# Attention block with Fourier layer: the values' bias added on ScalarE instead of GpSimd

## The chip, the cores and the metric

The kernel runs on one core of a Trainium2 chip, as one launch. The metric is the device time of that launch in microseconds (us); several runs are taken and their median is compared. One execution is also recorded by the hardware profiler. The engines of a core are named as in the profile: PE (TensorE, its weight loads PEld), DVE (VectorE), ACT (ScalarE), POOL (GpSimd) and SP (SyncE, which here only issues transfers). Each engine works through its own queue in order and waits at semaphores for the others.

## The reference

The input is an image of 48 x 48 tokens with 768 channels. The first layer is a transformer block with 12 heads of 64 channels and relative positions, the second a Fourier layer on blocks of 96 channels. Cut to what matters here:

```python
xn  = layernorm(x)
qkv = xn @ qkv_w + qkv_b                    # q, k, v: 12 heads, 2304 tokens, 64 channels
attn = (q * scale) @ k.T + rel_h[..., None] + rel_w[..., None, :]
out = softmax(attn) @ v                     # 12 x 2304 x 64
x   = x + out @ proj_w + proj_b
x   = x + gelu(layernorm(x) @ mlp_w1 + mlp_b1) @ mlp_w2 + mlp_b2
# second layer: rfft2, two small block matrices with relu and softshrink, irfft2, plus x
```

The bias of the values is not added to the values. As the weights of a softmax sum to one, it is added to the finished output of attention: `softmax(attn) @ (v + b) = softmax(attn) @ v + b`. This addition is what the change moves.

## The kernel before, in words

All arithmetic is in float32. The kernel has these stages: normalisation with queries, keys and values (up to about 402 us in the profile), attention (402 to 1471 us), projection (to about 1609 us), the two layers of the MLP (to about 2628 us) and the Fourier layer (to the end). A general form of attention stands in a branch for inputs whose sums overflow; it isn't executed here.

**Attention.** Heads are taken in six pairs (`pr`), queries in six chunks of 384 (`c`), so there are 36 chunks, counted 0 to 35 in this document (chunk 6 is `pr` 1, `c` 0). A chunk works as follows.

- For each of 18 tiles of 128 keys, PE makes the scores of both heads into a bank `sp` of PSUM, of which there are three (L678 for the content, L687 for the position), and ACT writes their exponentials into `main` (L697, the activation function Exp). DVE adds the exponentials up in `pairs` two tiles at a time (L871), and at the end in `acc` (L875).
- Then PE multiplies the exponentials with the values into `op` (L710), in six steps of three key tiles. Between the steps the function `between` puts other work, in an order written out by hand (`work[0]` to `work[5]`).
- Part of this work is for later chunks. `relative` makes the row terms of the position for a chunk three ahead; `columns` makes the column terms of the next pair. Both go through `two_parts`: two copies on ACT (L248, L249) and a subtraction on DVE (L250). `in_columns` copies queries on ACT (L702). Each `relative` then issues 24 transfers on SP's queue (L317, L321) that fill the tile `terms`. There is one such set in chunks with `c` from 0 to 2 and `c` = 4, and two sets where `c` = 5; the last pair needs fewer.
- The rest is for the denominators. In step 1 DVE turns and sums `acc` into `part` (L728, L730). In step 4 PE adds up over the partitions (L739), DVE takes the reciprocal `rden` (L741, two buffers) and adds to `sums` (L742), and POOL adds `rden` to `inverse` (L743), by which overflow is recognised later. In step 5 SP writes `rden` to `den_d` in DRAM (L757), stores a finished chunk, whose product was made in the chunk before, (`stored`, L791), and spreads the denominators of the chunk before over the partitions by two transfers, `spread` (L770). DVE then multiplies the output of two chunks before by its `spread` into `o` (L782, two buffers), and the bias is added to `o` (L785).
- After the last step ACT copies `op` to `ot` (L751), and the exponentials of the next chunk follow in its queue.

The orders of ACT, DVE and POOL in attention and those of PE and SP are the program's own (`manual_schedule`); nothing is reordered by a scheduler.

**POOL's other work.** During attention POOL also prepares the weights of the MLP: 48 pieces, two a chunk. A piece is a load into the single buffer `seven` (`asked`, L802, issued on POOL's own queue), four additions or subtractions of 128 x 192 (`left` or `right`, L164 to L167 or L175 to L178) and a store to `w1_d` or `w2_d` (L815). POOL's order within a chunk is: load (`kt == 2`), sums and store (`kt == 12`), load (step 1), `inverse`, bias, sums and store (end of the chunk). The function that is changed, and the one that orders its place:

```python
4: [partial(inverses, pr, c)],
5: [partial(left_apart, pr, c), stored],
...
work[5] += [partial(spread_out, 1), partial(scaled, 1)]
```

Of the kernel before, what the change touches and what calls it, by code (L numbers as in the profile page):

```python
# [13 lines left out]
AF = mybir.ActivationFunctionType  # L14
ALU = mybir.AluOpType
# [27 lines left out]
V_LN1G, V_LN1B, V_LN2G, V_LN2B, V_QB, V_KB, V_VB, V_B1 = 0, 6, 12, 18, 24, 30, 36, 42  # L43
# [4 lines left out]
def block_then_afno(  # L48
# [27 lines left out]
    nc = tc.nc  # L76
# [15 lines left out]
    def col(i):  # L92
        return vec[:, i : i + 1]
# [102 lines left out]
    def by_rows(a):  # L196

        return a.rearrange("p (h b w) -> p b h w", h=8, b=3, w=16)

    def by_blocks(a):  # L200
        return a.rearrange("p (b h w) -> p b h w", h=8, b=3, w=16)

    with ExitStack() as flag_scope:
# [12 lines left out]
        with ExitStack() as att:  # L216
# [121 lines left out]
            def queries_keys_values(qkv):  # L338
# [263 lines left out]
                for p in range(T // TB):  # L602
# [13 lines left out]
                    for n, (kind, i) in enumerate(orders[p]):  # L616
                        if p < 2:
                            q = p + 1
                            if n in (5, 6):
                                hooks += [partial(centred, q, 3 * (n - 5) + c) for c in range(3)]  # L620
                            if n in (6, 7):
                                hooks[:0] = [partial(scaled, q, 3 * (n - 6) + c) for c in range(3)]
                            if n == 8:
                                hooks += [partial(token_sum, q, j) for j in range(4)]
# [36 lines left out]
            with tc.manual_schedule(engines={mybir.EngineType.PE, mybir.EngineType.SP}):  # L661
# [114 lines left out]
                def scaled(keep):  # L776

                    while len(to_scale) > keep:
                        pr, c, spread = to_scale.pop(0)
                        (ot,) = made.pop((pr, c))  # L780
                        o = o_pool.tile([P, G], F32, name="o")
                        nc.vector.tensor_tensor(  # L782
                            by_rows(o), by_blocks(ot), by_blocks(spread), ALU.mult
                        )
                        nc.gpsimd.tensor_scalar(o, o, col(V_VB + pr), None, ALU.add)  # L785
                        results.append((pr, c, o))

                def stored(queue=nc.sync):
# [28 lines left out]
                def between(pr, c, acc):  # L817

                    last = pr == NC - 1
                    work = {  # L820
                        1: [asked, partial(denominators, pr, c, acc)],
                        4: [partial(inverses, pr, c)],
                        5: [partial(left_apart, pr, c), stored],
                    }
                    if last and c > 2:
                        work[5] += [partial(spread_out, 0), partial(scaled, 1), stored]
                    else:
                        work[5] += [partial(spread_out, 1), partial(scaled, 1)]
                    if c < 3:
                        work[0] = [partial(relative, pr, c + 3)]  # L830
                    elif not last and c < 5:
                        for n in range(3):
                            work.setdefault(n, []).append(partial(columns, pr + 1, 3 * (c - 3) + n))
                        if c == 4:
                            work[3] = [partial(relative, pr + 1, 0)]
                    elif not last:
                        work[0] = [partial(relative, pr + 1, 1)]
                        work[2] = [partial(relative, pr + 1, 2)]
                    if not last and c in (2, 3):
                        for n in range(3):  # L840
                            i = 3 * (c - 2) + n
                            work.setdefault(n + (1, 3)[c - 2], []).append(
                                partial(in_columns, pr + 1, i)
                            )
                    return work
# [199 lines left out]
        with tc.If(safe < 1):  # L1045
            with ExitStack() as att:
# [27 lines left out]
                for pr in range(NC):  # L1074
# [12 lines left out]
                    for g in range(T // G):  # L1087
                        kp = psum.tile([P, G], F32, name="g_kp", tag="m")
                        for c in range(NC):
# [5 lines left out]
                            bias=kb[0:64, pr : pr + 1], scale=HD**-0.5,  # L1095
# [18 lines left out]
                    for sg in range(T // SG):  # L1114
# [4 lines left out]
                        for i in range(2):  # L1119
                            qp = psum.tile([P, G], F32, name="qp", tag="m")  # L1120
                            for c in range(NC):
# [6 lines left out]
                                bias=vec[0:64, V_QB + pr : V_QB + pr + 1],  # L1128
# [154 lines left out]
    with ExitStack() as mlp:  # L1283
        bias = mlp.enter_context(tc.tile_pool(name="mlp_const", bufs=1))
# [576 lines left out]
```

## Time and profile before

| | |
|---|---|
| median of 3 runs | 2881.7 us (2877.34 to 2889.69) |
| the profiled execution's own time | 2885.64 us |
| its span | 2883.8 us |
| granted clock of TensorE, mean | 0.991 |
| PE busy in the span | 2797.0 us (97%) |
| DVE busy | 1723.1 us (60%) |
| ACT busy | 920.0 us (32%) |
| POOL busy | 694.3 us (24%) |
| attention, first exponential to last copy `ot` | 403.7 to 1471.4 us |
| weight sums on POOL, first load to last store issued | 402.9 to 1187.6 us |

The span is the time from the first to the last recorded instruction. A busy share is an average over all stages; it does not say where an engine is waited for. The lists of waits say this: each line names an engine and a line that stood idle, then what released it, then the total in us, how often, and the longest. In the timelines a line gives the start, the duration, engine, source line and operation, and in brackets the idle time before it with its releaser. What is inferred there is the last event before the start; for a wait on several things it can name the wrong one. SPq lines are transfers issued by SP: their times are those of the issue, not of the transfer.

### The profile page before, as it was taken

The numbers are of one execution on the slowest core, as the hardware profiler recorded it, in microseconds if no ns is written. First come the engines' busy times: TensorE is split into PE (matmuls) and PEld (weight loads), VectorE is DVE, ScalarE is ACT, GpSimd is POOL, SyncE is SP. The second block draws the span as 40 slices with busy tenths as digits, with TensorE's granted clock in tenths as the row PEclk, the third lists the DMA queues.
The fourth block names the chain that finished last, engine by engine and source line by source line (L and its number), as shares of the span: only waits on it lengthen the run. The fifth ranks groups of instructions, "written<-read, shape, count | busy, mean of one in ns | idle before, by whom it ended". The sixth has DMA issues, their size and how long they took to land. (4 is left out here: it accounts for less than half of the span.)

```text
span 2883.8 us, 40970 instructions
## 1 busy us (share of the span) xinstructions
PE 2797.0 (97%) x15759; PEld 1717.5 (60%) x15759; DVE 1723.1 (60%) x2520; ACT 920.0 (32%) x1466; POOL 694.3 (24%) x662
## 2 busy tenths in 40 slices
PE   8999999999999899799999999999999999999998
PEld 4555655555656455465555555555555555556887
DVE  5434247667766566576766656675665556566665
ACT  1101136656656465475521210121110211112332
POOL 3405024445434344300045010011000100002433
PEclk9999999999999999899999999999999999999999
DMA  5535387585875867737352223223322322323254
GB/s 164 167 113 175 83 176 174 126 183 131 159 178 134 186 137 144 166 64 110 84 189 78 81 103 115 105 98 109 115 81 111 140 96 78 114 97 118 61 160 140
DMA packets 230716, 363.46 MB, mean 126 GB/s; under 512 B 26180, under 2 KB 203964, under 8 KB 224368
## 3 DMA queue, kind: packets, MB, share of 16 engines
q1 hardware_dynamic: 215720, 306.80, 40.2%
q0 software_dynamic: 12352, 52.11, 5.7%
q8 instruction: 127, 2.08, 0.3%
q10 hardware_dynamic: 2440, 1.84, 0.2%
q14 instruction: 77, 0.63, 0.1%
HBM read 211.59 MB, written 85.35 MB: 103 GB/s over the span
## 5 line engine op out<-in xcount | busy, mean ns | idle before, releaser
L697 ACT ACTIVATE main<-sp 128x768 f32<-128x768 f32 x648 | 516.3, 812 | 34.5 <-PE sp L687 19.3
L1320 PE MATMUL h<-shared,w 128*128 128x384 f32 x1512 | 504.1, 486 | 0.7 <-issue 0.7
L871 DVE TENSOR_TENSOR pairs<-pairs,main 128x1536 f32<-128x1536 f32 x252 | 461.7, 1832 | 27.1 <-DVE pairs L871 0.9
L687 PE MATMUL sp<-terms,select 64*128 64x384 f32 x1296 | 411.8, 629 | 0.0
L1320 PEld LDWEIGHTS h<-shared,w 128*128 128x128 f32 x1512 | 287.0, 190 | 202.0 <-issue 2.5
L1380 DVE TENSOR_TENSOR main<-o,main 128x384 f32<-128x384 f32 x540 | 299.1, 557 | 38.3 <-PE o L1378 0.2
L678 PE MATMUL sp<-shared 64*128 64x384 f32 x1296 | 264.6, 485 | 1.6 <-ACT row_hi L249 1.0
L678 PE MATMUL sp<-qT,kT 64*128 64x384 f32 x1296 | 264.2, 484 | 0.0
L1378 PE MATMUL o<-w,hs 128*128 128x384 f32 x648 | 262.6, 487 | 1.4 <-DVE hs L165 1.0
L1378 PE MATMUL o<-w,hT 128*128 128x384 f32 x648 | 245.2, 487 | 3.0 <-DVE main L1380 3.0
L1395 POOL TENSOR_TENSOR main<-main,acc 128x384 f32<-128x384 f32 x9 | 11.4, 1266 | 924.6 <-DVE main L1380 665.2
L710 PE MATMUL op<-main,shared 128*64 128x384 f32 x1296 | 222.7, 495 | 0.0
L710 PE MATMUL op<-main,v 128*64 128x384 f32 x1296 | 222.3, 496 | 0.0
L1326 ACT ACTIVATE hT<-c,vec 128x384 f32<-128x384 f32 x108 | 66.4, 615 | 465.2 <-DVE c L1332 465.1
L1332 DVE TENSOR_TENSOR c<-h,u 128x384 f32<-128x384 f32 x108 | 60.2, 558 | 212.8 <-PE h L1320 212.8
L871 DVE TENSOR_TENSOR pairs<-main 128x1536 f32<-128x1536 f32 x36 | 63.7, 1769 | 192.0 <-ACT main L697 192.0
L1378 PEld LDWEIGHTS o<-w,hT 128*128 128x128 f32 x648 | 122.7, 190 | 90.1 <-DVE main L1380 6.2
L1378 PEld LDWEIGHTS o<-w,hs 128*128 128x128 f32 x648 | 122.5, 190 | 89.4 <-DVE main L1380 4.8
L687 PEld LDWEIGHTS sp<-terms,select 64*128 64x128 f32 x1296 | 124.9, 186 | 84.1
L537 PE MATMUL m<-main 128*128 128x384 f32 x504 | 164.6, 488 | 2.2 <-DVE main L187 1.2
L710 PEld LDWEIGHTS op<-main,v 128*64 128x64 f32 x1296 | 99.1, 139 | 95.1 <-issue 71.5
L710 PEld LDWEIGHTS op<-main,shared 128*64 128x64 f32 x1296 | 98.1, 139 | 91.1 <-issue 67.1
(205 smaller groups left out, 3679.4 us busy)
## 6 DMA issues: line engine op xcount, KB each, us to landing
w<-w_d SPq DMA_DIRECT2D x72, 1344.0 KB
w_d<-seven POOLq DMA_DIRECT2D x48, 672.0 KB, 5.6
terms<-col_parts SPq DMA_DIRECT2D x432, 72.0 KB
seven<-in_w_blocks_dram POOLq DMA_DIRECT2D x48, 384.0 KB, 4.7
terms<-row_hi SPq DMA_DIRECT2D x216, 72.0 KB
terms<-row_lo SPq DMA_DIRECT2D x216, 72.0 KB
main<-in_qkv_w_dram SPq DMA_DIRECT2D x36, 384.0 KB
z<-zt SPq DMA_DIRECT2D x48, 192.0 KB
```

Source lines behind the costliest of these rows:

```text
L537: nc.tensor.matmul(bank, a[:, c, :], b[:, c, :], start=(first and c == 0), stop=(c == 2), skip_group_check=not first,)
L678: nc.tensor.matmul(sp[:, j, :G], kT[at, ts(kt, P)], qT[at, ts(c, G)], start=first, stop=not first,)
L687: nc.tensor.matmul(sp[:, j, :G], select[at, a % 2], ready[pr, c][at, a // 2, b], start=first, stop=not first,)
L697: nc.scalar.activation(p, sp[:, :, :G], AF.Exp, scale=HD**-0.5)
L710: nc.tensor.matmul(op[ts(j, 64)], v[:, kt, ts(j, 64)], exps[:, kt, j, :], start=(kt == 0), stop=(kt == NT - 1),)
L871: nc.vector.tensor_tensor(pairs, so_far, exps[:, ds(kt - 1, 2)], ALU.add)
L1320: nc.tensor.matmul(bank[i], a[:, c, :], b[:, c, :], start=(start and c == 0), stop=(c == 2), skip_group_check=not start,)
L1326: nc.scalar.activation(h[:, i, ts(k, G)], src, AF.Gelu, bias=col(V_B1 + tiles_of_chunk(n)[i]))
L1332: nc.vector.tensor_tensor(t, src, other, ALU.add)
L1378: nc.tensor.matmul(bank[k], a, b, start=start, stop=True, skip_group_check=not start)
L1380: nc.vector.tensor_tensor(dst, bank[k], dst, ALU.add)
L1395: nc.gpsimd.tensor_tensor(x12, x12, acc[i], ALU.add)
```

## The change

One line of the function `scaled`. The addition of the bias to the tile `o` (128 x 384, in place, one value of bias per partition) is now an activation with the function Identity on ACT; before it was a `tensor_scalar` on POOL. It stays at the same place of the program, so it stands in ACT's queue behind the copies of `two_parts` in that chunk and ahead of the copy `ot` (L751). In chunks with `c` 2 or 3 one of the copies of `in_columns` comes behind it as well. The orders of PE, DVE and SP are the same as before; the store of `o` waits for ACT and no longer for POOL.

```diff
                         nc.vector.tensor_tensor(
                             by_rows(o), by_blocks(ot), by_blocks(spread), ALU.mult
                         )
-                        nc.gpsimd.tensor_scalar(o, o, col(V_VB + pr), None, ALU.add)
+                        nc.scalar.activation(o, o, AF.Identity, bias=col(V_VB + pr))
                         results.append((pr, c, o))
```

## The prediction

> **What bounds the kernel now.** I read the page first: TensorE is busy for 97% of the span, and the chain that ended last is PE nearly throughout, but that chain reaches back only to 1532 us. The change lies earlier, in attention (402 to 1471 us), so I went on to the waits of each engine in 400 to 1490 us, and then to the timelines of POOL, SP, DVE and ACT there. First the page, then the waits (columns: total us, times, longest us):
>
> ```profile
> PE 2797.0 (97%) x15759; PEld 1717.5 (60%) x15759; DVE 1723.1 (60%) x2520; ACT 920.0 (32%) x1466; POOL 694.3 (24%) x662
> ...
> ```
> ```profile
> SPq L791 <- POOL o L785: 127.2, 13, 25.4
> SPq L757 <- DVE sums L742: 83.5, 6, 19.7
> ...
> POOL seven L802 <- DMA w_d<-seven: 245.0, 47, 10.0
> POOL seven L175 <- DMA seven<-in_w_blocks_dram: 82.9, 23, 7.6
> POOL seven L164 <- DMA seven<-in_w_blocks_dram: 82.5, 23, 6.7
> ...
> DVE o L782 <- DMA spread<-den_d: 75.6, 14, 19.6
> DVE rden L741 <- POOL inverse L743: 20.3, 5, 5.3
> ...
> PE small L739 <- DVE part L730: 33.2, 8, 16.7
> PE small L280 <- ACT col_parts L249: 10.2, 2, 5.2
> ```
>
> Read from the top: SP stands 127 us in front of the store of a finished chunk because GpSimd has not yet added its bias. SP is in order, so the spreading of the next inverse denominators and the score terms stand behind it; then DVE waits for `spread`, and PE for DVE's partial sums. One instance, from the timelines of POOL, SP and DVE:
>
> ```profile
> 1115.11 1.26 POOL L785 TENSOR_SCALAR o<-o,vec 128x384 f32<-128x384 f32 x1
> 1116.40 0.33 SPq L791 DMA_DIRECT2D oT<-o  x1
> 1147.02 0.35 DVE L741 RECIPROCAL rden<-small 24x32 f32<-24x32 f32 x1 [3.98 <-POOL inverse L743]
> 1160.96 1.13 SPq L770 DMA_DIRECT2D spread<-den_d  x2
> 1166.97 0.56 DVE L782 TENSOR_TENSOR o<-ot,spread 128x384 f32<-128x384 f32 x1 [19.56 <-DMA spread<-den_d]
> ...
> 1181.56 0.27 POOL L743 TENSOR_TENSOR inverse<-inverse,rden 24x32 f32<-24x32 f32 x1
> ```
>
> Number the 36 chunks 0 to 35. The copies `ot<-op` on ACT end each chunk; their distances are its length. Undisturbed it is 27.5 to 28.3 us, 29.0 where c = 3 and 30.3 where c = 4. Five chunks are longer: 7 (32.1), 15 (36.7), 19 (40.2), 21 (36.7) and 25 (46.4 us). Their excess is 4.4 + 7.7 + 12.5 + 7.7 + 18.7 = 51 us. This is all that can be gained here; the rest of the span is as it was.
>
> Why GpSimd is late: it does 48 pieces of weight sums, two a chunk, each one load, four operations and one store in a single buffer. They run from 403 to 1188 us, 16.5 us each, 33 a chunk against PE's 28.5. The sum `inverse` (L743) of chunk 0 is 0.4 us behind its `rden`, that of chunk 13 is 61 us behind. From there `rden`, which has two buffers, waits for the `inverse` of two chunks before: 832.8 after 832.5, 925.3 after 925.0, 1024.2 after 1023.9, 1147.0 after 1146.7.
>
> **The change, part by part.**
> Removed from POOL: 36 additions of 1.26 us (median; 2.8 when DVE's additions run beside them), 45 us. Each stands between the issue of a load (L802) and the first sum that needs it, and in 46 of 48 pieces that sum waits for the load (the L175 and L164 rows). So this frees almost none of POOL's time; only twice did the piece start the moment the bias ended (699.4 and 1184.5 us). I count 0; without that cover it would be up to 1.3 us a chunk.
>
> Added to ACT: 36 activations. The nearest row is L1326, the same tile with a bias from `vec`: 615 ns; so 22 us. They stand after the chunk's two-part copies and before `ot<-op`. There ACT waits 3.4 to 29.8 us for PE (its 34 waits are 311.8 us in all), so in itself this is 0. The Trainium skill's page "ScalarE: Activation LUTs" has a rule that could speak against it (What ACT_TABLE_LOAD costs): a switch of table set costs about 2.66 us. The trace has one table load of 1283 ns before attention's first exponential (402.4 us) and none later in it. Were Identity outside that set, two switches a chunk would cost 36 x 2 x 1.28 = 92 us by the trace's row, 192 by the page. The same page (Table sets) says that cheap functions lie in every set, and the changed instruction order has as many table loads as before. I take 0.
>
> Moved wait: no DMA is added or moved; 35 stores stay on SP and one on POOL, and they now wait for ACT. Bias k now follows DVE's product k directly, a chunk before its store's place in SP's queue. So the 127 us go. What is late next on SP is `den_d` (L757), which waits for `rden`, and so for `inverse`: this second tie to GpSimd's queue stays.
>
> New wait: the bias on ACT waits for DVE's product (L782); behind it stand `ot<-op` and the next 18 exponentials, and behind those PE's scores, with three banks. With M the time of the PE product L739, undisturbed chunks show: `rden` at M + 0.34, product at M + 0.66 to 1.22, `ot<-op` at M + 4.2, first exponential at M + 5.2. With the bias it can start at M + 0.66 + 0.56 + 0.62 + 0.4 = M + 2.3. So the product may be 2.9 us late free of charge; DVE's chain has about 0.4 us more, so lateness beyond 3.3 us is paid by PE in full. Before, late `rden` or product had some 8 us of slack in DVE's additions. What is behind the new wait is thus more sensitive.
>
> The sum, (i) with POOL's times held as in the trace. M grows by the undisturbed length plus max(0, lateness - 3.3); lateness is the later of `inverse`(c-2) and SP's backlog. The backlog exists at c = 0, after two sets of terms in one chunk: measured 10.2 us at chunk 6 and 2.3 at chunk 30, where SP never waited for POOL; I take 6 between. Chunk 6 costs 6.9 us (4.4 before), chunk 12 costs 2.7: M(13) = 805.7, M(16) = 892.8, M(17) = 921.0. Then the additions are 0.7, 3.6, 4.5, 7.3, 0, 0, 3.4, 3.7 and 7.3 for chunks 17 to 25, against lateness 4.0, 6.9, 7.8, 10.6, 3.1, 1.1, 6.7, 7.0 and 10.6; M(26) = 1206.0. In the trace it is 1217.2: 11.2 us gained. The extra cost at chunk 6 is absorbed, since GpSimd sets the pace later.
>
> (ii) POOL's times need not hold. The four operations of a piece take 2.5 us when DVE is not in its additions of pairs, 8.2 us wholly under them (0.59 and 1.99 us each). The page "SBUF — State Buffer" (SBUF: two separate sides) calls the port that both use an exclusive lock, the loser blocked for a whole instruction. By it each of the four pays up to one addition, 1.83 us, so 2.4 + 7.3 = 9.7; the trace's 8.2 decides. Without the waits for `spread`, DVE's additions stand earlier against POOL's second piece of a chunk. Moving both in turn along chunks 13 to 23, these pieces become 4.5, 7.8, 8.2, 4.2, 5.8, 2.5, 5.4, 7.1, 5.5, 5.2, 3.5 us (59.7) for 4.5, 7.8, 8.2, 4.7, 7.2, 6.0, 5.4, 7.4, 8.2, 6.9, 6.8 (73.1): 13.4 us, with which M(26) = 1192.6. The gain is between 11.2 and 24.6. As loads (3.2 to 8.2 us) and stores (4.5 to 10.9 us) scatter, I count two thirds of the 13.4: 20 us. PE alone, with the costs at chunks 6 and 12, would reach M(26) = 1175, a gain of 42.
>
> After chunk 26 the sums are done and nothing changes: at chunk 30 the lateness 2.3 is within 3.3.
>
> The profiled execution took 2885.6 us (span 2883.8 and 1.8 around it): 2885.6 - 20 = 2865.6. It lies 3.9 above the median of 2881.7; against the median the forecast is 2861.7, say 2862.
>
> **The rivals.**
> *GpSimd's pace still sets everything* (25%). The bias leaves that queue but `inverse` does not, so the change takes away one of two ties to it. For: the four pairs of times above, 0.3 us apart. Against: the two longest excesses, chunks 19 and 25, follow waits for `spread` of 14 and 20 us, not for `inverse`. The time is (i): 2881.7 - 11 = 2870.5.
>
> *ACT stands in front of a late product* (17%), slower. Place: the first exponentials of the next chunk. Price: lateness beyond 3.3 us at each chunk, if `spread` stays as late as now because it was SP's own issue of terms (0.63 us each) and not the store that held it. With the trace's lateness, chunks 6 to 30 pay 6.9 + 2.3 + 5.3 + 3.0 + 15.3 + 0.3 + 5.4 + 1.2 + 19.9 = 59.6 us (chunks 6, 12, 14, 17, 18, 19, 20, 23 and 24). Of it 35.6 is paid today at chunks 7, 19 and 25: 24 us net, 2906. It decides as soon as the mean lateness stays near today's; about half of it breaks even. Against: SP had no wait of its own at chunk 6, and in chunks 8 to 23 it mostly stands right behind the bias.
>
> *No tie left* (within the first case): GpSimd falls in step with PE, 42 us, 2840.
>
> **How the numbers follow.** First case 58%, centre 2862, from 2840 to 2867; GpSimd's pace 25%, from 2864 to 2880; ACT's wait 17%. What a measurement can tell from no change is about 0.5%, 14.4 us. Faster by more: nearly all of the first case and a fifth of the second, 60%. Within: 23%. Slower: most of the third, 17%. The range from 2836 to 2896 leaves out the third case's far part and a little at the low end.
>
> **What would show it.** L785 on ACT, 36 times near 0.6 us; SP's wait at L791 from 127 us to a few; DVE's wait for `spread` well under 75.6 us; chunks 15 and 21 at 29 us, no chunk above 38; DVE's wait for `inverse` larger, not smaller; POOL's last piece before 1187.6 us. Were L751's predecessor on ACT, the bias, to wait over 3 us in most chunks, with the exponentials starting late behind it, the third case would be true; were POOL's last piece at 1188 or later, the second.

## The result and the profile after

The changed kernel takes 2889.9 us (median of 18 runs, 2882.2 to 2900.5); the kernel before takes 2882.9 us (18 runs beside it). The ratio is 1.0026, with a 95% interval of 1.0013 to 1.0039: slower by about 7.5 us, where 20 us less were forecast. A second series gave 1.0033 (1.0016 to 1.0050).

The profiled execution after took 2883.8 us (span 2882.0), near the fast end of its runs and 2 us under the record before (2885.6). I therefore use a second record of the same kernel too, called *again* below: it took 2900.0 us (span 2898.2), among the slower ones. The median lies between the two. First the busy row of the page after, and the row of the added instruction (durations in ns: least, median, most):

```profile
PE 2803.0 (97%) x15759; PEld 1720.7 (60%) x15759; DVE 1722.7 (60%) x2520; ACT 944.7 (33%) x1502; POOL 658.6 (23%) x626
```

```profile
L785 ACT ACTIVATE o<-o,vec x36: 617/617/617, 483.1 to 1472.6; 128x384 f32<-128x384 f32 x36
```

ACT gained 36 instructions of 617 ns (22 us, as counted), POOL lost 36. Now the lists of waits of the kernel after, 400 to 1490 us, for SP, DVE, PE and ACT (total us, times, longest):

```profile
SPq L317 <- ACT row_hi L249: 146.5, 17, 26.8
SPq L757 <- DVE sums L742: 124.4, 8, 21.6
...
DVE rden L741 <- POOL inverse L743: 56.5, 9, 12.6
DVE o L782 <- DMA spread<-den_d: 24.5, 6, 10.0
...
PE sp L678 <- ACT main L697: 36.9, 11, 8.2
PE small L739 <- DVE part L730: 0.6, 2, 0.4
...
ACT o L785 <- DVE o L782: 261.2, 36, 20.1
ACT ot L751 <- PE op L710: 69.0, 26, 11.4
```

SP's 127 us in front of the store are gone from the list: 1.6 us in front of it are left for ACT's bias. DVE waits for `spread` 25 us instead of 76. PE no longer waits for DVE's `part` (33 us before), but 37 us for ACT's exponentials, which hardly occurred before (0.6 us). DVE waits almost three times as long for GpSimd's `inverse`, and ACT now stands 261 us in front of DVE's product, most of it time in which it stood in front of PE's `op` before. So the wait was removed as intended, and two others took its place.

The excess of each chunk up to 26 over its undisturbed length (where it is over 1 us), from the distances of the copies `ot`, in us:

| kernel | chunks | sum |
|---|---|---|
| before | 7: 4.3; 15: 7.7; 19: 12.4; 21: 7.7; 25: 18.6 | 51 |
| after | 6: 7.3; 12: 5.0; 18: 3.5; 19: 8.7; 20: 5.1; 21: 1.2; 23: 2.8; 24: 8.1; 25: 6.3 | 48 |
| again | 6: 7.8; 12: 4.9; 13: 1.1; 15: 2.7; 17: 3.9; 18: 10.6; 19: 8.5; 20: 3.9; 21: 5.5; 24: 4.6; 25: 9.3; 26: 1.0 | 64 |

A few long stalls became many short ones. The end of chunk 25 in the record after shows how, by the timelines of POOL, DVE and ACT:

```profile
1186.75 0.55 POOL L802 DMA_DIRECT2D seven<-in_w_blocks_dram  x1 [7.70 <-DMA w_d<-seven]
1187.31 0.27 POOL L743 TENSOR_TENSOR inverse<-inverse,rden 24x32 f32<-24x32 f32 x1
1193.16 2.22 POOL L175 TENSOR_TENSOR seven<-seven 128x192 f32<-128x192 f32 x1 [5.58 <-DMA seven<-in_w_blocks_dram]
1195.45 2.06 POOL L176 TENSOR_TENSOR seven<-seven 128x192 f32<-128x192 f32 x1
...
1187.61 0.34 DVE L741 RECIPROCAL rden<-small 24x32 f32<-24x32 f32 x1 [7.60 <-POOL inverse L743]
1187.93 0.53 DVE L782 TENSOR_TENSOR o<-ot,spread 128x384 f32<-128x384 f32 x1
1193.16 1.76 DVE L871 TENSOR_TENSOR pairs<-main 128x1536 f32<-128x1536 f32 x1 [4.70 <-ACT main L697]
...
1188.50 0.62 ACT L785 ACTIVATE o<-o,vec 128x384 f32<-128x384 f32 x1 [14.97 <-DVE o L782]
1189.38 2.21 ACT L697 ACTIVATE main<-sp 128x768 f32<-128x768 f32 x3
```

Read it as one chain. GpSimd reaches `inverse` of chunk 23 at 1187.31, behind the issue of its last load. DVE's `rden` of chunk 25 follows 0.3 us later, then the product, then the bias on ACT, and only then the next chunk's exponentials. DVE's additions start 5.6 us after `inverse`, at the very moment at which the load has landed and GpSimd starts its own sums: each takes 2.0 to 2.2 us instead of 0.59. In the record before, the piece behind `inverse` of chunk 22 is as quiet as can be; DVE's product waits for `spread` until 1166.97 there, and its additions come after it:

```profile
1146.72 0.27 POOL L743 TENSOR_TENSOR inverse<-inverse,rden 24x32 f32<-24x32 f32 x1
1153.69 0.59 POOL L164 TENSOR_TENSOR seven<-seven 128x192 f32<-128x192 f32 x1 [5.47 <-DMA seven<-in_w_blocks_dram]
1154.36 0.59 POOL L165 TENSOR_TENSOR seven<-seven 128x192 f32<-128x192 f32 x1
1155.03 0.59 POOL L166 TENSOR_TENSOR seven<-seven 128x192 f32<-128x192 f32 x1
1155.58 0.59 POOL L167 TENSOR_TENSOR seven<-seven 128x192 f32<-128x192 f32 x1
```

From here on, *first piece* is the one summed ahead of a chunk's `inverse` in GpSimd's queue, *second piece* the one behind it.

### The profile page after: what moved, and what is told of

Read it like the earlier page. It is cut to its first block, busy times and chain, and to the rows that moved or that the text cites. A ratio compares the mean times of both kernels' runs of the same rounds, so it can differ in the third digit from the quotient of the medians.

```text
span 2882.0 us, 40848 instructions
## 1 busy us (share of the span) xinstructions
PE 2803.0 (97%) x15759; PEld 1720.7 (60%) x15759; DVE 1722.7 (60%) x2520; ACT 944.7 (33%) x1502; POOL 658.6 (23%) x626
## 5 line engine op out<-in xcount | busy, mean ns | idle before, releaser
L687 PE MATMUL sp<-terms,select 64*128 64x384 f32 x1296 | 417.9, 639 | 0.0
L678 PE MATMUL sp<-shared 64*128 64x384 f32 x1296 | 270.4, 494 | 18.6 <-ACT main L697 17.6
L1395 POOL TENSOR_TENSOR main<-main,acc 128x384 f32<-128x384 f32 x9 | 11.4, 1264 | 924.2 <-DVE main L1380 665.3
L678 PEld LDWEIGHTS sp<-qT,kT 64*128 64x128 f32 x1296 | 119.4, 189 | 73.2 <-ACT main L697 24.4
L678 PEld LDWEIGHTS sp<-shared 64*128 64x128 f32 x1296 | 120.0, 190 | 71.3 <-ACT main L697 21.9
```

The lines of the kernel that those rows point to most:

```text
L678: nc.tensor.matmul(sp[:, j, :G], kT[at, ts(kt, P)], qT[at, ts(c, G)], start=first, stop=not first,)
L687: nc.tensor.matmul(sp[:, j, :G], select[at, a % 2], ready[pr, c][at, a // 2, b], start=first, stop=not first,)
```

## The experiments

Each ratio is to the kernel before, run beside it on the same chip; the chip is not the same for all rows. *Theory A*: GpSimd's 48 pieces set the pace of chunks 14 to 25 through the two buffers of `rden`, and ACT now hands that lateness to the exponentials. The theory marked A2 from the second group on adds that GpSimd itself becomes slower without the old wait.

| kernel | median us | ratio to before (95%) |
|---|---|---|
| again (the changed kernel) | 2892.8 | 1.0033 (1.0016 to 1.0050) |
| eight buffers for `rden`, changed kernel | 2864.5 | 0.9935 (0.9919 to 0.9951) |
| eight buffers for `rden`, kernel before | 2881.7 | 0.9994 (0.9986 to 1.0002) |
| bias late on ACT | 2893.2 | 1.0033 (1.0017 to 1.0048) |
| late bias and eight buffers | 2849.2 | 0.9888 (0.9872 to 0.9904) |
| before, no weight additions | 2837.3 | 0.9839 (0.9826 to 0.9853) |
| changed, no weight additions | 2863.4 | 0.9933 (0.9917 to 0.9949) |
| changed, second piece ahead of `inverse` | 2904.4 | 1.0068 (1.0049 to 1.0087) |
| no bias at all | 2892.0 | 1.0035 (1.0023 to 1.0046) |
| before, stores on POOL's queue | 2892.4 | 1.0035 (1.0021 to 1.0049) |
| late bias, eight buffers, early spread | 2852.7 | 0.9901 (0.9884 to 0.9918) |
| the same with three buffers for `o` | 2848.2 | 0.9869 (0.9852 to 0.9885) |
| tie without work (bias on one column) | 2877.8 | 0.9985 (0.9976 to 0.9995) |
| the kernel before once more | 2881.1 | 1.0008 (0.9994 to 1.0022) |

**The changed kernel once more.** No edit.

> The changed kernel once more, for a second profiled execution and its time beside the others. Theory A (GpSimd's pieces set the pace of chunks 14 to 25 through the two buffers of rden, and the bias now hands that lateness to the exponentials): ratio to before 1.000 to 1.005, ACT's wait for DVE's product some 260 us, PE's wait for the exponentials 30 to 45 us, the last piece on GpSimd at 1195 to 1215 us. Theory B (chance of one recorded execution): these waits differ by more than half between the two records.

The waits are alike in both records: ACT in front of the product 261 and 276 us, PE in front of the exponentials 37 and 51, and GpSimd's last store is issued at 1202.1 and 1215.4 us (1187.6 before). In its waits, the record after is not an odd one.

**Cutting one tie: eight buffers for `rden`,** in the changed kernel and in the kernel before.

```diff
-                    rden = o_pool.tile([ND, 32], F32, name="rden")
+                    rden = o_pool.tile([ND, 32], F32, name="rden", bufs=8)
```

> The changed kernel with eight buffers for rden in place of two, so that the reciprocal no longer waits for GpSimd's sum two chunks back. Theory A: DVE's wait for inverse (56 us) goes to 0, chunks 18 to 25 fall to 28 to 31 us, and only the c = 0 chunks still pay for the late spread (7 us each at chunks 6, 12, 18, 24): 20 to 35 us under before, about 2850 to 2862. Theory B (what ACT waits for is the spread's transfer and SP's backlog): the wait moves to the spread, time within 5 us of the changed kernel, 2885 to 2893.

> The kernel before (bias on GpSimd) with eight buffers for rden. Theory A with two ties to GpSimd's queue (rden's buffers, and the store that waits for the bias): one is cut, the other holds, SP still waits over 100 us for the bias; 0 to 12 us under before, 2870 to 2883. If the buffers of rden were the only tie that matters: 35 to 45 us under before, 2838 to 2848.

Theory A for both, though the first falls just short of its range: it is 19 us under the kernel before, and 28 us under the changed kernel; the kernel before wins nothing. In the first the wait for `inverse` is gone, and what stays are chunks 6, 12, 18, 24 and 25 (8.3, 6.2, 2.1, 5.6 and 1.5 us). In the second the store still ties SP to GpSimd; waits of SP and DVE in this kernel:

```profile
SPq L791 <- POOL o L785: 111.4, 11, 24.6
...
DVE o L782 <- DMA spread<-den_d: 115.3, 18, 19.7
```

So there were two ties, each enough to hold the whole. Cutting the one that the change cuts leaves the other, and the reverse.

**Bias on ACT, but not in front of the exponentials.** The product goes into a list; the activation is issued in step 0 of the next chunk.

```diff
-                        nc.scalar.activation(o, o, AF.Identity, bias=col(V_VB + pr))
-                        results.append((pr, c, o))
+                        products_made.append((pr, c, o))
+                def biased():
+                    while products_made:
+                        pr, c, o = products_made.pop(0)
+                        nc.scalar.activation(o, o, AF.Identity, bias=col(V_VB + pr))
+                        results.append((pr, c, o))
...
+                    work.setdefault(0, []).append(biased)
```

> Bias on ACT, but issued a chunk later, behind the next chunk's 18 exponentials and two-part copies, rden with two buffers: ACT stands in front of no product. Theory A: ACT's wait for the product goes from 261 us to under 10, and lateness is again absorbed by some 8 us of slack in DVE's additions, but GpSimd's pace holds through rden: 5 to 15 us under before, 2868 to 2878. If ACT's wait were the whole loss: 30 us or more under before, 2855 or less. If SP's wait for the bias had never cost anything: within 4 us of before.

All three expectations failed. ACT's wait for the product did fall, to 26 us, but the time did not: DVE's wait for `inverse` grew to 133 us, and PE waits 44 us for `part` again:

```profile
DVE rden L741 <- POOL inverse L743: 133.4, 12, 20.7
...
PE small L739 <- DVE part L730: 44.1, 11, 10.6
...
ACT o L792 <- DVE o L783: 25.5, 4, 9.0
```

With the tie through `rden` in place, ACT's queue is thus not what keeps the changed kernel behind the kernel before. I had to look at GpSimd's own times, which I had taken as given (table further down): it reaches `inverse` of chunk 23 at 1200.0 us here, at 1181.6 before.

**Both.** Late bias and eight buffers.

> Both ties cut: bias on ACT a chunk later (behind the next exponentials) and eight buffers for rden. Theory A2 (GpSimd's end of its last piece sets the end of chunk 25 through rden; ACT's wait is a second, smaller loss of some 22 us at chunks 6, 12, 18 and 24): neither is left, only DVE's own wait for the late spread, about 4 us at chunks 7 and 13: 30 to 40 us under before, 2843 to 2853, under the kernel with eight buffers alone by 10 to 20 us. Rival (ACT's wait costs nothing that DVE would not cost in the same place): as eight buffers alone, 2860 to 2868.

As expected: 34 us under before, 15 us under eight buffers alone (14 by the two ratios). ACT's place in front of the product therefore costs about 15 us once GpSimd doesn't hold the kernel. The waits of DVE that are left:

```profile
DVE pairs L879 <- ACT main L697: 226.1, 33, 7.9
DVE o L783 <- DMA spread<-den_d: 48.6, 10, 11.2
```

This version beats both kernels, though GpSimd's last store is as late as 1229.9 us: nobody waits for it in attention.

**Without the weight additions,** for the kernel before and the changed one: `seven` is made once and set to zero, the loads and stores stay, the calls of `left` and `right` are left out.

```diff
-                    (left, right)[k](
-                        nc.gpsimd, *(seven[:, a] for a in range(4)), [seven[:, a] for a in (4, 5, 6)]
-                    )
```

> The kernel before with the four additions of each weight piece left out on GpSimd (loads and stores stay; the weights of the MLP are then wrong). Theory A2: a piece takes 12 to 13 us, two fit into a chunk, GpSimd never falls behind, no tie acts: 35 to 45 us under before, 2838 to 2848. If it were the loads and stores that set GpSimd's pace: within 10 us of before.

> The changed kernel with the same additions left out. Theory A2: no lateness of GpSimd to wait for, and nothing gained by taking the bias from it; ACT still stands in front of the product that waits for its spread at chunks 6, 12, 18 and 24: 12 to 22 us above the kernel before without the additions, 2852 to 2866. Rival (the moved bias costs nothing by itself): equal to it within 4 us.

`inverse` is never more than 3.5 us behind its `rden` here, where it was up to 67 us before (last store at 1089 and 1105 us). The kernel before comes to 2837, just under the range expected, which bounds what GpSimd's lateness costs it at 46 us. Between the two kernels lie 26 us for the moved bias by itself; 12 to 22 were expected. The timeline of ACT at chunk 6 without the additions, changed kernel:

```profile
610.67 0.61 ACT L785 ACTIVATE o<-o,vec 128x384 f32<-128x384 f32 x1 [20.12 <-DVE o L782]
611.55 2.21 ACT L697 ACTIVATE main<-sp 128x768 f32<-128x768 f32 x3
```

ACT has stood idle for 20 us; the exponentials of chunk 7 start some 9 us late, because `spread` is issued behind 48 transfers of terms in SP's queue (568.7 to 603.0 us) and DVE's product waits 12 us for it. Chunks 6, 12, 18 and 24 pay 9.3, 6.5, 5.9 and 2.6 us. This is the rival of the prediction that ends slower, at the place that it named.

**The second piece ahead of `inverse`,** changed kernel.

```diff
-                        4: [partial(inverses, pr, c)],
+                        4: [summed, partial(inverses, pr, c)],
...
                             finish(pr, c, op)
-                            summed()
```

> The changed kernel with the chunk's second weight piece ahead of the sum inverse in GpSimd's queue and no longer behind it. Theory A2 (the end pieces became slow because DVE's additions now follow right behind inverse and hold the port): the second pieces of chunks 13 to 23 fall from 47 to 49 us in sum to 25 to 35, and GpSimd issues its last store 10 to 20 us earlier, near 1190; as inverse itself stands later in its queue, the time gains less, 0 to 12 us under the changed kernel, 2878 to 2892. Rival (their slowness is chance, not the place): sum of second pieces 40 to 55 us as before, same time.

The first half holds: the second pieces of chunks 13 to 23 take 29.6 us in sum, so their slowness depends on the place in the queue and is no chance. The rest failed: the first pieces of these chunks now meet DVE's additions, 81.1 us instead of 64.0 and 52.9 in the two records, GpSimd's last store comes at 1206 us, and since `inverse` stands behind it, the kernel is slower, at 2904. Here the collisions moved from one piece to the other; the sum of both hardly changed (110.7 against 111.2 in the record after).

**No bias at all,** and **stores on POOL's queue,** from the kernel before.

```diff
-                        nc.gpsimd.tensor_scalar(o, o, col(V_VB + pr), None, ALU.add)
```

```diff
-                def stored(queue=nc.sync):
+                def stored(queue=nc.gpsimd):
```

> The kernel before with the addition of the values' bias left out altogether (no bias on any engine; the inputs' bias is zero). Theory A2 (what slows the changed kernel is that GpSimd's pieces take longer once SP and DVE no longer wait behind the bias, and that the end of its last piece sets the end of chunk 25): although 45 us of work are gone, as slow as the bias put late on ACT, 2884 to 2896, last piece stored at 1200 to 1220 instead of 1188. Rival (ACT's activations or the place in its queue are the whole loss): 10 to 30 us under before, 2853 to 2873.

> The kernel before with the stores of finished chunks issued from GpSimd's queue instead of SP's; the bias stays on GpSimd. Theory A2: SP no longer waits for the bias, DVE's wait for the spread falls from 76 us to 20 to 45, and GpSimd's last piece ends later than 1188 (35 issues of its own more, and more collisions): 2884 to 2905. Rival (the gain of a free SP is real and only ACT's wait spoilt it): 10 us or more under before, 2873 or less.

Taking 45 us of work away makes the kernel 9 us slower than before, just as moving it does. The loss against before is thus there without any activation. The DVE and POOL timelines without the bias, at the end of chunk 25:

```profile
1197.38 0.34 DVE L741 RECIPROCAL rden<-small 24x32 f32<-24x32 f32 x1 [19.51 <-POOL inverse L743]
1198.16 1.74 DVE L870 TENSOR_TENSOR pairs<-main 128x1536 f32<-128x1536 f32 x1
1200.00 13.83 DVE L870 TENSOR_TENSOR pairs<-pairs,main 128x1536 f32<-128x1536 f32 x7
...
1199.83 0.59 POOL L175 TENSOR_TENSOR seven<-seven 128x192 f32<-128x192 f32 x1 [2.49 <-DMA seven<-in_w_blocks_dram]
1200.51 1.99 POOL L176 TENSOR_TENSOR seven<-seven 128x192 f32<-128x192 f32 x1
```

Freed by `inverse`, DVE starts its additions at once, under GpSimd's next piece. With the stores on POOL the time came out as expected, but not by the way expected: the last piece came early (1179 us), and DVE's product now waits for one of the two buffers of `o`, whose stores stand in GpSimd's queue. In each of chunks 7 to 24 the product starts within 0.1 us of the landing of the store of the product two before. That makes it a third tie to the same queue.

**Tie without work, and the kernel before once more.** What was still open: whether GpSimd is faster in the kernel before because of the tie, or by chance.

```diff
-                        nc.gpsimd.tensor_scalar(o, o, col(V_VB + pr), None, ALU.add)
+                        nc.gpsimd.tensor_scalar(o[:, :1], o[:, :1], col(V_VB + pr), None, ALU.add)
```

> The kernel before with the bias added on GpSimd to the first of the 384 columns of a finished chunk alone (the other columns get none; the inputs' bias is zero): the tie of SP's store to GpSimd's queue stays, the work goes. Theory A2 (the tie, by holding DVE back, lets GpSimd's pieces run faster): as the kernel before, 2879 to 2886, last piece stored at 1183 to 1195 us. Rival (the four records without the tie were late by chance, or the bias's work itself matters): as with no bias at all, 2888 to 2896, last piece after 1200.

> The kernel before once more, for a second record. Theory A2: ratio 1.000, last piece stored at 1183 to 1195 us, the sum inverse of chunk 23 at 1178 to 1190. Rival (chance): last piece anywhere from 1185 to 1215.

With the tie and next to no work (297 ns an instruction) the time is 2878, slightly below the range named in advance; without bias and without tie it is 2892. Its ratio of 0.9985 also prices the work that was taken from POOL, with the tie left as it was: about 4 us. SP and DVE wait in it as in the kernel before:

```profile
SPq L791 <- POOL o L785: 126.9, 13, 24.5
...
DVE o L782 <- DMA spread<-den_d: 94.0, 19, 14.0
```

The table puts the records with two buffers for `rden` side by side, with the eight-buffer kernel before, which has the same tie. M(26) is the start of L739 in chunk 26, as in the prediction; the sums of pieces are first and second pieces of chunks 13 to 23, from the start of their first operation to the end of the fourth, worked out from POOL's timeline, in us. The column behind them counts in how many of the 11 second pieces one of DVE's additions of pairs runs.

| record | tie of the store | pieces, first + second | additions in second | `inverse` of 23 | `rden` of 25 | M(26) |
|---|---|---|---|---|---|---|
| before | yes | 72.9 + 30.0 | 0 of 11 | 1181.6 | 1188.0 | 1217.2 |
| before, once more | yes | 74.2 + 28.5 | 0 of 11 | 1185.6 | 1187.9 | 1216.8 |
| tie without work | yes | 74.7 + 27.7 | 0 of 11 | 1184.1 | 1185.6 | 1215.0 |
| before, eight buffers | yes | 73.7 + 29.1 | 0 of 11 | 1185.2 | 1186.7 | 1216.7 |
| after | no | 64.0 + 47.2 | 7 of 11 | 1187.3 | 1187.6 | 1212.6 |
| again | no | 52.9 + 49.2 | 8 of 11 | 1203.9 | 1204.2 | 1230.1 |
| late bias | no | 32.0 + 84.1 | 11 of 11 | 1200.0 | 1200.3 | 1220.3 |
| no bias | no | 28.6 + 81.4 | 11 of 11 | 1197.1 | 1197.4 | 1217.3 |

With the tie, DVE mostly stands in front of its product when GpSimd sums a second piece (behind eight of the 11 in the record before), waiting for `spread`. None of its additions of pairs runs during these pieces, and they stay close to their least, 27.5 us in sum. Without the tie DVE's additions follow `inverse` closely and take that quiet time away. The other records without the tie that keep the order of pieces, with eight buffers for `rden` or with the stores on POOL, have additions in 4 to 10 of the 11. In return `rden` binds directly: M(26) is 31 to 36 us behind `inverse` with the tie, 20 where the bias is late or absent, and 25 to 26 where it stands on ACT. GpSimd is later, the way from it to M(26) is shorter, and the two nearly cancel.

One part stays open. In *again* the pieces' own sums are no longer than before (102.1 against 102.9); its lateness comes from its 48 loads (from issue to the first sum) and 47 stores (from issue to the next load), which take 254 and 298 us in sum against 238 and 289 before. Why these transfers were slower there, no run separates. That an execution of the changed kernel is slower than one of the kernel before is thus explained only in part: in the record after M(26) is even 4.6 us earlier than before.

**An early spread.** On top of late bias and eight buffers, `spread_out` goes to the start of the chunk, ahead of the terms; then also a third buffer for `o`.

```diff
-                        work[0] = [partial(relative, pr, c + 3)]
+                        work[0] = [partial(spread_out, 0), partial(relative, pr, c + 3)]
...
-                        o = o_pool.tile([P, G], F32, name="o")
+                        o = o_pool.tile([P, G], F32, name="o", bufs=3)
```

> Bias late on ACT, eight buffers for rden, and the spread of the chunk before issued at the start of a chunk, ahead of its score terms in SP's queue. Theory A2: DVE's wait for the spread goes from 49 us to under 10 and the chunks at c = 0 and 1 lose their last 2 to 6 us each: 5 to 12 us under the kernel with late bias and eight buffers, 2836 to 2845. Rival (those waits are hidden there already): 2847 to 2852.

> The early spread again, with a third buffer for o, since in the run before DVE's wait only moved from the spread to the store of o (49 us of waits for oT). Theory A2: with that wait gone the chunks run at their undisturbed lengths apart from column terms: 5 to 10 us under late bias with eight buffers, 2839 to 2845. Rival (what is left in these chunks is not DVE's wait): 2847 to 2853.

Neither gained clearly: the intervals of both overlap that of late bias with eight buffers. In the first the wait moved from `spread` to the store of `o` (49 us). In the second this is gone too, and chunks 9, 15 and 27 are 5 to 7 us too long instead: PE and DVE wait for the column terms, which can't be written over until the transfers that still read them are done.

```profile
DVE col_parts L250 <- DMA terms<-col_parts: 9.6, 2, 5.7
...
PE small L280 <- ACT col_parts L249: 11.9, 3, 4.5
```

Late bias with eight buffers for `rden`, at 0.9888 about 34 us under the kernel before, is the simplest version that reaches this; the third buffer's 0.9869 can't be told from it.

## Why the prediction was wrong

It forecast 20 us less; 7.5 us more came out, by the following steps.

Right: 617 ns for each activation, that no table load comes in, that SP's 127 us go, that DVE's wait for `spread` falls, that `inverse` stays as a second tie with a longer wait, and the price of a late product at chunk 6 (6.9 us; measured 7.3 and 7.8). Less so at chunk 12: 5.0 and 4.9 us for 2.7. The step from `rden` of chunk 25 to M(26) comes to 24.1 us in (i) and is 25.0 and 25.9. The work taken from POOL was put at 0 and is worth about 4 us (tie without work).

The step that failed is the one called (ii), and with it the 1181.6 us for `inverse` of chunk 23 on which (i) stands. Its eleven lengths (73.1 us, to become 59.7) are those of the first pieces, though its text says second. These did fall, from 72.9 to 64.0 and 52.9 us. For the pieces behind `inverse` the sum has no term, as if their 2.5 us were given; they rose from 30.0 to 47.2 and 49.2, because their quiet time was a product of the very wait that the change removes. Up to `inverse` of chunk 23 this rise is 11.4 and 16.4 us (the last second piece comes after it), against 8.9 and 20.0 won on the first pieces: of the gain forecast for the pieces, hardly anything is left.

With the rest of GpSimd's queue, `inverse` came 5.7 and 22.3 us later than held, and M(26) at 1212.6 and 1230.1 instead of 1206.0 by (i), or 1197.2 by the 20 us forecast. These 15.4 and 32.9 us are nearly all by which the two executions missed 2865.6 (18.2 and 34.4 us); the remainder is lost behind chunk 26, where nothing was to change. Putting the measured `inverse` into (i) gives about 1206.0 + 5.7 = 1211.7 and 1228.3: the recurrence was good, its input was not. Of the 22.3 us in *again*, though, the pieces explain nothing; these are the slower loads and stores, whose cause stays open.

Of the rivals, the one of GpSimd's pace named the mechanism, and its sign came: POOL's last piece is stored at 1202.1 and 1215.4 us, not before 1188. But its time was (i), with GpSimd's pace unchanged and 11 us won. The one of ACT in front of a late product is true as a mechanism and worth about 15 us (late bias, with eight buffers) to 26 us (no weight additions) where GpSimd doesn't bind. Where it does bind it is covered: there the late bias gains nothing, and no bias at all loses as much against before as the changed kernel. Its sign, a bias that waits over 3 us in most chunks, came too (27 and 28 of 36), but it tells little: most of this is time in which ACT waited for PE's `op` before, and PE waits for the exponentials only 11 and 12 times.

By the Trainium skill's page "SBUF — State Buffer" (SBUF: two separate sides), with the loser blocked for a whole instruction, the prediction's estimate for a piece wholly under DVE's additions was 9.7 us. Pieces took up to 8.5 us in these records, so the trace was again the better guide. The larger error was where in time the collisions fall, not their size.

## What to carry to other kernels

A wait on a slow queue may come through several ties, here a store and the buffers of a small tile; find all of them before cutting one, since the second takes over. When a shared resource sets the pace, its quiet times may come from the very stalls that you remove, so retime all of its work and not only the part that moves in your favour. An operation that waits for a late producer belongs behind the work of its queue that others wait for, even where it is as short as 0.6 us.

## What the runs showed that I had not expected

Leaving out 36 instructions with their wait made a kernel slower (2892 against 2883 us), and shrinking them to one column while keeping the wait made it faster than that by 14 us (2878). The second pieces of chunks 13 to 23 sum to 27.7 to 30.0 us in all four records with the tie and to 47 to 84 in the four of the table without it: in each kernel the engines settle into a step with one another, and when GpSimd gets its quiet time depends on that step.
